# Attention plus ternary feed-forward on one core: the exchange of the values through DRAM in six transfers, two loads and two sums a step sooner

## Chip, core and metric

The kernel runs on one core of one Trainium2 chip. The metric is the device time of one execution in microseconds (us), as the median of several runs. The core has five engines, each with its own in-order queue: TensorE (PE in the profile, its weight loads PEld), VectorE (DVE), ScalarE (ACT), GpSimd (POOL) and SyncE (SP), which here only issues transfers. ACT and POOL issue transfers too. All transfers share 16 DMA engines. An instruction that must wait for a semaphore holds everything behind it on its engine.

## What is computed

```python
def reference(x, Wqkv, Wout, w1, w2, w3):          # x: 1 x 2048 x 256, float32
    xn = layernorm(x)
    q, k, v = heads(einsum('bsd,ed->bse', xn, Wqkv))      # 16 heads of 128
    w = softmax(einsum('bqhd,bkhd->bhqk', q, k) * 128 ** -0.5)
    attn = einsum('bse,de->bsd', einsum('bhqk,bkhd->bqhd', w, v), Wout)
    qz = lambda w: clip(round(w / (mean(abs(w)) + 1e-8)), -1, 1)
    ffn = (sigmoid(xn @ qz(w1).T) * (xn @ qz(w2).T)) @ qz(w3).T
    return x + attn + ffn
```

The factor on the logits makes the softmax sharp, so everything in the attention is in float32.

## The kernel before

**Order of the work.** Layernorm, the first projections and the whole feed-forward come first (about 140 us). Then one loop runs over 64 *blocks*: 16 heads times 4 blocks of 512 queries. A *group* is two heads, so eight blocks; below, i (0 to 7) is the block's number in its group and t (0 to 3) its quarter, and "step (i, t)" names a place in the loop. The order on every engine is written out by hand, step after step; no scheduler moves anything.

**One step.** Each step makes the scores of one tile of 128 queries six steps ahead (`scores`: 16 matmul rows in the trace, maxima on DVE L632, exponentials on ACT L642), moves the exponentials across partitions in 16 transfers (`exchanged`, L661, ten on SP's queue and six on ACT's), turns them in 32 x 32 squares on DVE (`transposed`, L708) and so fills slots of the big tile R. Beside that it computes a quarter of the product of weights and values for block n (`weighted`, L775) and one or two 512-column products for the next heads' projections.

**The product of weights and values** is done by Winograd's scheme for a 2 x 2 partition with 7 products, so sums and differences of both operands are needed. Those of the weights are `differences` on POOL (L728): T1a and T3a of block n+1 in step (n, 3), T1b and T3b in (n, 0), T2l (lower half of the slot) at the end of (n, 0), T2h (upper half) and T4 at the beginning of (n, 1). Quarter 1 of the product reads T1 and T2; its lower half of k needs T2l, its upper half T2h. Those of the values are made once per head by `v_combined` (L750): sums 0 and 1 in step (n, 0) of the head's first block, after T1b and T3b; sums 2 and 3 in (n, 2). Quarter 1 reads sums 0 and 1, quarter 2 reads sum 2.

**Values for the next group.** In blocks 4 to 7 the values of the next two heads are made transposed, half a head at a time, on PE and DVE (L308, L315). To turn them, `v_exchanged` (L317 to L326) moves a half (128 x 1024 numbers, 0.5 MB) across groups of 32 partitions into a scratch area `v_part` (two 128 x 512 pieces, part of the tile xnT), and `v_transposed` (L328 to L333) turns 32 x 32 squares on DVE from there back into the value tile. The same scratch area serves all four halves of a group, so the next exchange has to wait for the turning of the one before. `between` (L1006 to L1048) places these calls at the end of a step: exchanges of the first head at (5, 1) and (7, 1), turned at (5, 3) and (7, 3); exchanges of the second at (5, 3) and (7, 3), turned at (6, 1) and at (0, 1) of the next group.

**Output sums.** The projected output of all heads is accumulated in DRAM tiles `yds`; two of them at a time are loaded into `osums` (`y_moved`, L839), added to on DVE (`fast_o_read`, L911) and stored back. `o_moved` (L846) runs at the end of steps 0 to 3 of blocks 0 to 3 and loads the first of a pair at (0, 0) and (2, 0); the addition that first needs it is in step (0, 1) and (2, 1).

**Other POOL work at these places.** At the beginning of each block `put_away` (L829) stores the finished block from oT, which DVE writes at L803; `spread` (L687) reloads oT with the reciprocals at (n, 1), `inverses` (L680) stores them at (n, 2) in four transfers.

Of the kernel before, what the change touches and what calls it, by code (L numbers as in the profile page):

```python
# [9 lines left out]
F32 = mybir.dt.float32  # L10
# [10 lines left out]
def layernorm_attention_bitffn_kernel(  # L21
# [14 lines left out]
    nc = tc.nc  # L36
    P = 128
    S, DM = x.shape
# [5 lines left out]
    QB = 512  # L44
    NB = S // QB
# [248 lines left out]
    def v_half(h: int, half: int):  # L294
        return v_tile(h)[:, half * NKT // 2 : (half + 1) * NKT // 2]
# [21 lines left out]
    def v_exchanged(h: int, half: int):  # L317

        v = v_half(h, half).rearrange("p k d -> p (k d)")
        for j in range(P // 32):  # L320
            for q in range(P // 32):
                queue = nc.sync if q % 2 else nc.gpsimd
                queue.dma_start(  # L323
                    v_part[q // 2][bass.ts(j, 32), bass.ts(q % 2, S // 8)],
                    v[bass.ts(q, 32), bass.ts(j, S // 8)],
                )  # L326

    def v_transposed(h: int, half: int):  # L328
        v = v_half(h, half).rearrange("p k (q r) -> p q k r", r=32)
        for u in range(2):  # L330
            nc.vector.transpose(  # L331
                v[:, 2 * u : 2 * u + 2], v_part[u].rearrange("p (q k r) -> p q k r", q=2, r=32)
            )  # L333

    wxs, v_part = {}, [xnT[:, 0, bass.ts(c, QB)] for c in (1, 3)]
# [9 lines left out]
    away = ctx.enter_context(tc.tile_pool(name="away", bufs=1, space=bass.MemoryType.DRAM))  # L345
# [2 lines left out]
        [away.tile([P, QB], F32, tag=f"od{h}_{c}", name=f"od{h}_{c}") for c in range(NB)]  # L348
        for h in range(2 * G)
    ]  # L350
    rds = [away.tile([TB, P], F32, tag=f"rd{i}", name=f"rd{i}") for i in range(2)]


# [255 lines left out]
    blocks = [(h, b) for h in range(H) for b in range(NB)]  # L609
# [74 lines left out]
    def spread(n: int):  # L684

        if n < NBK - NB:
            nc.gpsimd.dma_start(oT, rds[n % 2].rearrange("t p -> (t p)").partition_broadcast(P))  # L687
            rbs[n] = oT
# [3 lines left out]
    for n in range(1, len(blocks)):  # L692
        a, b, c, d, e = roles[-1]
# [19 lines left out]
    def differences(n: int, what: str):  # L713

        a, b, c, d, e = roles[n]
        todo, where = what[:2], what[2:]
        o, x, y = {"T1": (e, c, a), "T2": (a, d, e), "T3": (c, d, c), "T4": (b, b, a)}[todo]
        o, x, y = (R[:, i] for i in (o, x, y))
        if where in ("a", "b"):
            t = "ab".index(where)  # L720
            o, x, y = (i[:, t * S // 2 : (t + 1) * S // 2] for i in (o, x, y))
        elif where in ("l", "h"):
            k = "lh".index(where)
            o, x, y = (
                i.rearrange("p (t k q) -> p t k q", t=2 * NQ, q=32)[:, :, k * KH // 2 : (k + 1) * KH // 2]
                for i in (o, x, y)
            )
        nc.gpsimd.tensor_tensor(o, x, y, ALU.subtract)  # L728
# [3 lines left out]
    def v_parts(h: int):  # L732
        if h not in vparts:
            v = v_tile(h)
            k0, k1 = v_place(h, 0), v_place(h, KH)
            ls = [[v[:, k : k + KH, c * HP : (c + 1) * HP] for k in (k0, k1)] for c in range(2)]
            st = apool.tile([P, 3, KH, HP], F32, tag="st", name=f"st{h}", bufs=1)
            s3 = ls[1][0]
            if h == H - 1:
                s3 = wpool.tile([P, KH, HP], F32, tag="wq", name=f"s3{h}")  # L740
            vparts[h] = ls, st, s3
        return vparts[h]

    def v_combined(h: int, i: int):
        ((l11, l12), (l21, l22)), st, s3 = v_parts(h)
        o, x, y, op = (
            (st[:, 0], l21, l22, ALU.add), (st[:, 1], st[:, 0], l11, ALU.subtract),
            (s3, l11, l21, ALU.subtract), (st[:, 2], l12, st[:, 1], ALU.subtract),
        )[i]
        nc.gpsimd.tensor_tensor(o, x, y, op)  # L750
# [75 lines left out]
    def put_away(n: int):  # L826

        h, b = blocks[n]
        nc.gpsimd.dma_start(ods[h % (2 * G)][b], oT)  # L829
# [6 lines left out]
    def o_fetched(g: int, pair: int, i: int, head: int, c: int):  # L836
        nc.gpsimd.dma_start(o3[:, i], ods[(g * G + head) % (2 * G)][2 * pair + c])

    def y_moved(pair: int, c: int, back: bool):  # L839
        y, yd = osums[:, c], yds[2 * pair + c]  # L840
        nc.gpsimd.dma_start(*((yd, y) if back else (y, yd)))

    def o_difference(i: int, a: int, b: int):
        nc.gpsimd.tensor_tensor(o3[:, i], o3[:, a], o3[:, b], ALU.subtract)

    def o_moved(g: int, i: int, t: int):  # L846

        pair, more = i // 2, i == 1
        at = i % 2, t
        if at == (0, 0):  # L850
            o_difference(1, 2, 1)
            y_moved(pair, 0, False)
        elif at == (0, 1):
            o_difference(0, 1, 0)
        elif at == (0, 2):
            o_fetched(g, pair, 2, 1, 0)
        elif at == (1, 0):
            o_difference(2, 2, 1)
            if more:
                o_fetched(g, 1, 0, 0, 0)  # L860
        elif at == (1, 1):
            y_moved(pair, 1, True)
        elif at == (1, 2):
            if more:
                y_moved(1, 1, False)
                o_fetched(g, 1, 1, 0, 1)
            else:
                y_moved(pair, 0, True)
        elif at == (1, 3) and more:
            y_moved(pair, 0, True)  # L870
            o_fetched(g, 1, 2, 1, 1)
            o_difference(1, 1, 0)
# [125 lines left out]
    GB = G * NB  # L998
# [7 lines left out]
    def between(n: int, t: int):  # L1006

        g, i = divmod(n, GB)
        last = NBK - NB

        how = {
            (5, 1): (v_exchanged, 0, 0), (5, 3): (v_transposed, 0, 0), (6, 1): (v_transposed, 1, 0),
            (7, 1): (v_exchanged, 0, 1), (7, 3): (v_transposed, 0, 1),
        }.get((i, t))
        if t == 1:
            spread(n)
            if i == NB - 1 and g + 1 < H // G:
                load_weights(g + 1, "v", nc.gpsimd)
            elif i == GB - 1 and n < last or n == last - 1:
                load_weights(g, "o", nc.gpsimd)  # L1020
        if g and i < NB:
            o_moved(g - 1, i, t)
        elif n < last:
            o_begun(g, i, t)
        if how and g + 1 < H // G:
            how[0]((g + 1) * G + how[1], how[2])
        if n >= last - 1 and t == (1 if n < last else 2):
            b = n + 1 - last
            nc.gpsimd.dma_start(o3[:, b % 2], ods[(H - 2) % (2 * G)][b])
        if g and (i, t) == (0, 1):  # L1030
            v_transposed(g * G + 1, 1)
        if t == 2:
            if i == GB - 1 and n < last:
                wo = weights[g, "o"]
                sums_of(wo[:, :, :P], wo[:, :, P:], f"wos{g}")
        if t == 3:
            if i in (5, 7) and g + 1 < H // G:
                v_exchanged((g + 1) * G + 1, i // 2 - 2)
            if i == NB - 1 and g + 1 < H // G:
                v_sums(g + 1)  # L1040

        b, r = divmod(n * TB + t - ((last - 2) * TB + 1), TB)
        if r == 0 and 0 < b <= NB:
            x_added(b - 1)
        if r == 0 and 0 <= b < NB:
            turning_back(b)
        if r == 2 and 0 <= b < NB:
            turned_back(b)  # L1048

    behind = []  # L1050
    with tc.manual_schedule():
        for u in range(-LEAD, (NBK - 1) * TB):
            n, t = divmod(u, TB)
            v = u + LEAD
# [10 lines left out]
            g, i = divmod(n, GB)  # L1065
            if n >= NB and t < 2:
                i, j = divmod(i, NB)
                j = 2 * j + t
# [19 lines left out]
            if t == 0 and n >= 0:  # L1088
                if 0 < n <= NBK - NB:
                    put_away(n - 1)  # L1090
                differences(n, "T1b")
                differences(n, "T3b")
                if blocks[n][1] == 0:
                    v_combined(blocks[n][0], 0)
                    v_combined(blocks[n][0], 1)
            elif t == 1 and n >= 0:
                differences(n, "T2h")
                differences(n, "T4")
            elif t == 2 and n >= 0:
                if blocks[n][1] == 0:  # L1100
                    v_combined(blocks[n][0], 2)
                    v_combined(blocks[n][0], 3)
            elif t == 3 and -1 <= n < NBK - 2:
                differences(n + 1, "T1a")
                differences(n + 1, "T3a")
            if more:
                scores(v, late=beside)

# [62 lines left out]
        n = NBK - 1  # L1171
# [51 lines left out]
```

## Time and profile before

| | |
|---|---|
| runs | 2405.11, 2409.61, 2410.33 us; median 2409.61 |
| profiled execution | 2405.91 us, span 2403.9 us, mean granted TensorE clock 0.979 |
| busy: PE, POOL, DVE, ACT | 2208.7 (92%), 1824.2 (76%), 1889.2 (79%), 748.0 us (31%) |
| exchange of the values on POOL's queue | 224 issues, 498 ns each, 3.2 us to landing |
| the same on SP's queue | 224 issues, 589 ns each (median), 1.9 us to landing |
| scores start to scores start, steps t = 0 to 3 of block 0 | 13.95, 13.69, 13.02, 6.88 us |
| the same, block 1 | 8.60, 8.60, 8.60, 6.02 us |
| block 2 | 10.16, 9.95, 8.75, 8.82 us |
| block 4 | 8.60, 10.41, 9.77, 6.88 us |
| block 5 | 8.60, 7.75, 8.60, 6.02 us |
| block 6 | 8.72, 10.46, 8.67, 9.38 us |
| block 7 | 8.60, 7.87, 8.60, 6.93 us |

How to read it: the last seven rows are read from the timeline of TensorE as the time between the first score matmuls of neighbouring steps, averaged over blocks 8 to 55 (six groups). In these steps TensorE always has the same scores to do, quarters 0 to 2 of the product are equally long and quarter 3 is half as long; steps differ by at most one extra product of 0.86 us. So 8.60 (or 7.75 with one product fewer) and 6.02 to 6.88 us are steps in which TensorE ran without a gap, and what lies above that is waiting. Engines that are not TensorE may be idle without cost; a wait costs time where it ends up in one of these intervals.

### The profile page before, as it was taken

To read this page: it belongs to the slowest core of one execution; us is meant where nothing else is said; L and a number is where in the kernel's file an instruction comes from. 1 tells how busy PE (TensorE), PEld (TensorE's weight loads), DVE (VectorE), ACT (ScalarE), POOL (GpSimd) and SP (SyncE) were. 2 spreads that over 40 slices of the span, in tenths; PEclk is the share of its full clock that TensorE was granted. 3 is DMA by queue.
4 is the path that set the end of the run, shared out by engine and by line. 5 is a ranking of instruction groups with operands and counts; after the bars stand their busy time and mean duration, and the time that the engine had idled before them with its cause. 6 is when DMAs were issued, how large, how long until landed. Compare 5 with 4: busy or idle time off the path is not lost.

```text
span 2403.9 us, 41619 instructions
## 1 busy us (share of the span) xinstructions
PE 2208.7 (92%) x13386; PEld 1065.3 (44%) x13386; DVE 1889.2 (79%) x2578; ACT 748.0 (31%) x1390; POOL 1824.2 (76%) x1504
## 2 busy tenths in 40 slices
PE   9999999899989999899998999889997999989787
PEld 6644444444434544344443444344443444435345
DVE  6577788788878888788877888778887888878855
ACT  5533333233323333223332333223332333323321
POOL 0166877887797788788788778788778788878984
PEclk9999999999999999999999999999999999999989
DMA  2265656666666666576666766657666665657744
GB/s 85 69 146 149 154 145 175 161 179 166 157 172 184 176 152 163 151 195 174 154 160 153 199 162 153 169 155 184 167 164 154 186 174 149 162 153 190 197 125 126
DMA packets 256170, 383.81 MB, mean 160 GB/s; under 512 B 86224, under 2 KB 97936, under 8 KB 255952
## 3 DMA queue, kind: packets, MB, share of 16 engines
q1 hardware_dynamic: 138416, 182.30, 29.8%
q10 hardware_dynamic: 74896, 101.94, 16.7%
q0 software_dynamic: 42640, 96.92, 14.5%
q8 instruction: 105, 1.72, 0.3%
q14 instruction: 113, 0.93, 0.1%
HBM read 62.98 MB, written 34.73 MB: 41 GB/s over the span
## 4 chain that ended last, share of the span: by engine, by line
PE 28%; DMA 25%; POOL 15%; SPq 11%; DVE 11%; issue 7%; ACTq 2%; ACT 1%; DVEq 0%; POOLq 0%
DMA part<-p 23%; PE av L775 10%; POOL R L728 9%; PE s L94 8%; SPq L661 8%; DVE R L708 5%; SPq L323 3%; DVE mx L632 2%; PE pw L94 2%; POOL st L750 2%; ACTq L661 2%; PE ph L507 2%; DMA xnT<-v 1%; PE pow L94 1%; DVE oU L801 1%
## 5 line engine op out<-in xcount | busy, mean ns | idle before, releaser
L728 POOL TENSOR_TENSOR R<-R 128x1024 f32<-128x1024 f32 x441 | 1180.3, 2684 | 58.2 <-DVE R L708 24.3
L642 ACT ACTIVATE p<-s,nm 128x1024 f32<-128x1024 f32 x512 | 566.8, 1111 | 1458.9 <-DMA part<-p 986.4
L94 PE MATMUL s<-kT,qT 128*64 128x512 f32 x4000 | 926.3, 593 | 11.0 <-ACT p L642 10.9
L632 DVE TENSOR_REDUCE mx<-s 128x1 f32<-128x1024 f32 x512 | 612.2, 1216 | 141.5 <-PE s L94 128.0
L708 DVE STREAM_TRANSPOSE R<-part 128x1024 f32<-128x1024 f32 x512 | 605.7, 1221 | 124.4 <-DMA part<-p 116.4
L775 PE MATMUL av<-R,st 128*64 128x256 f32 x3024 | 515.2, 399 | 106.6 <-POOL R L728 67.1
L775 PE MATMUL av<-R,v 128*64 128x256 f32 x3728 | 553.3, 389 | 25.9 <-DVE oU L801 25.8
L94 PEld LDWEIGHTS s<-kT,qT 128*64 128x64 f32 x4000 | 307.8, 137 | 540.0 <-issue 474.1
L775 PEld LDWEIGHTS av<-R,st 128*64 128x64 f32 x3024 | 302.4, 144 | 320.0 <-POOL R L728 97.3
L775 PEld LDWEIGHTS av<-R,v 128*64 128x64 f32 x3728 | 343.8, 141 | 195.1 <-issue 62.7
L680 POOL DMA_DIRECT2D rd<-r x240 | 124.8, 527 | 135.8 <-DVE r L678 120.8
L911 DVE TENSOR_TENSOR osums<-pow,osums 128x512 f32<-128x512 f32 x196 | 126.0, 678 | 75.6 <-DMA osums<-yd 74.4
L829 POOL DMA_DIRECT2D od<-oT x60 | 34.5, 576 | 170.2 <-DVE oT L803 161.8
L323 POOL DMA_DIRECT2D xnT<-v x224 | 111.7, 505 | 58.3 <-DVE v L331 47.8
L801 DVE TENSOR_TENSOR oU<-av,oU 64x256 f32<-64x256 f32 x248 | 101.1, 408 | 38.0 <-PE av L775 20.1
L793 ACT COPY oU<-av 64x256 f32<-64x256 f32 x248 | 91.0, 367 | 124.5 <-PE av L775 120.4
L642 ACT ACTIVATION_READ_ACCUMULATOR p<-s,nm 128x1 f32 x512 | 100.0, 195 | 0.0
L94 PE MATMUL pw<-t,ws 128*64 128x512 f32 x336 | 94.2, 594 | 2.4 <-DVE kT L200 2.3
L160 POOL TENSOR_TENSOR t<-xnT 128x512 f32<-128x512 f32 x4 | 5.1, 1272 | 106.9 <-DMA part<-p 106.9
L315 DVE TENSOR_TENSOR v<-pvw,v 128x512 f32<-128x512 f32 x98 | 65.1, 676 | 20.6 <-PE pvw L94 20.6
L200 DVE TENSOR_TENSOR kT<-pw,kT 128x512 f32<-128x512 f32 x112 | 76.9, 687 | 1.8
L94 PE MATMUL pw<-xnT,wk 128*64 128x512 f32 x224 | 69.1, 596 | 5.5 <-DVE kT L200 5.2
(164 smaller groups left out, 1606.8 us busy)
## 6 DMA issues: line engine op xcount, KB each, us to landing
part<-p SPq DMA_DIRECT2D x2556, 64.0 KB, 2.2
part<-p ACTq DMA_DIRECT2D x1540, 64.0 KB, 2.3
oT<-rd POOLq DMA_DIRECT2D x60, 256.0 KB, 4.3
od<-oT POOLq DMA_DIRECT2D x60, 256.0 KB, 3.2
o<-od POOLq DMA_DIRECT2D x60, 256.0 KB, 3.8
osums<-yd POOLq DMA_DIRECT2D x28, 512.0 KB, 4.9
yd<-osums POOLq DMA_DIRECT2D x28, 512.0 KB, 4.5
xnT<-v POOLq DMA_DIRECT2D x224, 32.0 KB, 3.2
```

The source lines that it names most:

```text
L94: nc.tensor.matmul(out[c * HP : (c + 1) * HP], lhs[:, c * HP : (c + 1) * HP], rhs, start=start, stop=stop, skip_group_check=True,)
L323: queue.dma_start(v_part[q // 2][bass.ts(j, 32), bass.ts(q % 2, S // 8)], v[bass.ts(q, 32), bass.ts(j, S // 8)],)
L632: nc.vector.tensor_reduce(mx[:, i : i + 1], s, AX.X, ALU.max)
L642: nc.scalar.activation(p, s, AF.Exp, bias=nm, accum_out=sums[n][:, t, i : i + 1],)
L661: queue.dma_start(parts[v][g // 2][bass.ts(j, 32), g % 2, :], ps[j // 2][bass.ts(g, 32), bass.ts(j % 2, S // NQ)],)
L680: nc.gpsimd.dma_start(rds[n % 2][:, bass.ts(j, 32)], riT[32 * j : 32 * j + TB, :])
L708: nc.vector.transpose(to[:, t % 2, 2 * i : 2 * i + 2], part.rearrange("p g (s c) -> p g s c", s=2),)
L728: nc.gpsimd.tensor_tensor(o, x, y, ALU.subtract)
L775: nc.tensor.matmul(av[i * HP : (i + 1) * HP, half], l[:, kk], moving(s, kk), start=start, stop=(k == units[r] - 1), skip_group_check=True,)
L793: nc.scalar.copy(u[op, oq], av[ap, half])
L801: nc.vector.tensor_tensor(u[p, q], av[p, half], u[p, q], ALU.add)
L911: nc.vector.tensor_tensor(y, pm, y, ALU.add)
```

## The change

Three things are changed.

1. `v_exchanged` no longer makes 16 transfers of 32 KB inside SBUF (eight on SP's queue, eight on POOL's). It makes four stores of 128 KB into a new DRAM tile and two loads of 256 KB from it into the scratch area, all six on POOL's queue. A load needs two of the stores to have landed. Every call is one step earlier: exchanges of the first head at (5, 0) and (7, 0), turned at (5, 2) and (7, 2); exchanges of the second at (5, 2) and (7, 2); their turning stays at (6, 1) and (0, 1).
2. The load of the first output sum of a pair moves from the end of step (0, 0) or (2, 0) to its beginning, right behind `put_away` and ahead of T1b.
3. Sums 0 and 1 of a head's values move from (n, 0) to (n-1, 3), behind T1a and T3a, for every head but the first.

```diff
@@ v_exchanged
-        for j in range(P // 32):
-            for q in range(P // 32):
-                queue = nc.sync if q % 2 else nc.gpsimd
-                queue.dma_start(
-                    v_part[q // 2][bass.ts(j, 32), bass.ts(q % 2, S // 8)],
-                    v[bass.ts(q, 32), bass.ts(j, S // 8)],
-                )
+        vd = vds[half].rearrange("(j r) (q c) -> q r j c", r=32, c=S // 8)
+        for q in range(P // 32):
+            nc.gpsimd.dma_start(vd[q], v[bass.ts(q, 32)].rearrange("r (j c) -> r j c", c=S // 8))
+        for u in range(2):
+            nc.gpsimd.dma_start(v_part[u], vds[half][:, bass.ts(u, QB)])
@@ DRAM tiles
+    vds = [away.tile([P, S // 2], F32, tag=f"vd{i}", name=f"vd{i}") for i in range(2)]
@@ o_moved
+    def o_loaded(g: int, i: int):
+        if i % 2 == 0:
+            y_moved(i // 2, 0, False)
+
         if at == (0, 0):
             o_difference(1, 2, 1)
-            y_moved(pair, 0, False)
@@ between
-            (5, 1): (v_exchanged, 0, 0), (5, 3): (v_transposed, 0, 0), (6, 1): (v_transposed, 1, 0),
-            (7, 1): (v_exchanged, 0, 1), (7, 3): (v_transposed, 0, 1),
+            (5, 0): (v_exchanged, 0, 0), (5, 2): (v_transposed, 0, 0), (6, 1): (v_transposed, 1, 0),
+            (7, 0): (v_exchanged, 0, 1), (7, 2): (v_transposed, 0, 1),
...
-        if t == 3:
             if i in (5, 7) and g + 1 < H // G:
                 v_exchanged((g + 1) * G + 1, i // 2 - 2)
+        if t == 3:
@@ the loop over steps
             if t == 0 and n >= 0:
                 if 0 < n <= NBK - NB:
                     put_away(n - 1)
+                if n >= GB and n % GB < NB:
+                    o_loaded(n // GB - 1, n % GB)
                 differences(n, "T1b")
                 differences(n, "T3b")
-                if blocks[n][1] == 0:
+                if n == 0:
                     v_combined(blocks[n][0], 0)
                     v_combined(blocks[n][0], 1)
...
             elif t == 3 and -1 <= n < NBK - 2:
                 differences(n + 1, "T1a")
                 differences(n + 1, "T3a")
+                if n >= 0 and blocks[n + 1][1] == 0:
+                    v_combined(blocks[n + 1][0], 0)
+                    v_combined(blocks[n + 1][0], 1)
```

On POOL's queue the exchange at the end of (5, 0) and (7, 0) stands between T2l and T2h of that block; the one at (5, 2) and (7, 2) stands ahead of T1a and T3a of the next.

## The prediction

> **What bounds the kernel now.** I read the page first: TensorE is busy for 92% of the span and POOL for 76%, so neither a single engine nor the transfers set the pace everywhere. Then the list of waits, for those that name the lines of the change; its columns are who waited, for whom, us in total, times, longest.
>
> ```profile
> PE 2208.7 (92%) x13386; PEld 1065.3 (44%) x13386; DVE 1889.2 (79%) x2578; ACT 748.0 (31%) x1390; POOL 1824.2 (76%) x1504
> ```
>
> ```profile
> PEld av L775 <- POOL R L728: 97.3, 69, 4.6
> ...
> DVE osums L911 <- DMA osums<-yd: 74.4, 14, 9.3
> ...
> PEld av L775 <- POOL st L750: 55.7, 26, 11.6
> POOL xnT L323 <- DVE v L331: 47.8, 13, 6.1
> ...
> DVE v L331 <- DMA xnT<-v: 30.1, 13, 3.3
> ```
>
> All three parts aim at waits that exist: 74.4 us for the output sums, 55.7 for the sums of the values (`st`), 47.8 and 30.1 around the exchange. But DVE's and POOL's waits cost only what reaches TensorE. The step table shows where that is: block 0 loses 13.95+13.69+13.02 against 3 x 8.60, so 15 us; blocks 2, 4 and 6 a few each; blocks 5 and 7 run at full pace. So I followed one such change of heads, steps (23, 0) to (24, 2), on POOL's timeline (columns: start, us, what, count, idle time before it).
>
> ```profile
> 944.43 14.11 POOL L728 TENSOR_TENSOR R<-R 128x1024 f32<-128x1024 f32 x5
> ...
> 960.99 3.48 POOL L323 DMA_DIRECT2D xnT<-v  x7
> 965.26 0.50 POOL L323 DMA_DIRECT2D xnT<-v  x1 [0.79 <-DMA wo<-in_woutT_dram]
> 967.11 2.07 POOL L680 DMA_DIRECT2D rd<-r  x4 [1.36 <-DMA xnT<-v]
> ...
> 980.87 4.03 POOL L323 DMA_DIRECT2D xnT<-v  x8 [4.49 <-DVE v L331]
> ...
> 985.48 4.82 POOL L728 TENSOR_TENSOR R<-R 128x1024 f32<-128x1024 f32 x2
> 990.26 1.27 POOL L750 TENSOR_TENSOR st<-v 128x512 f32<-128x512 f32 x1
> ...
> 1006.89 1.26 POOL L750 TENSOR_TENSOR st<-v,st 128x512 f32<-128x512 f32 x1
> ```
>
> POOL hardly rests from 944.4 until `st` is complete at 1008.15: 63.7 us with 6.6 idle (0.79+1.36+4.49). TensorE waits for it at the end:
>
> ```profile
> 953.96 3.62 PE L775 MATMUL av<-R,st 128*64 128x256 f32 x32
> ...
> 981.68 5.36 PE L775 MATMUL av<-R,v 128*64 128x256 f32 x32 [3.87 <-DVE oU L801]
> ...
> 995.25 2.71 PE L775 MATMUL av<-R,st 128*64 128x256 f32 x16 [2.63 <-POOL R L728]
> 999.33 3.25 PE L775 MATMUL av<-R,st 128*64 128x256 f32 x13 [1.38 <-POOL R L728]
> ```
>
> So in block 0 POOL is the bound, and the 6.5 us that DVE waits for `osums` there run beside POOL's chain.
>
> **The exchange on POOL.** Before, its half costs eight issues, 4.0 us. After, four stores are issued at 0, 0.55, 1.10 and 1.65 us (the 0.55 to 0.58 of L841 and L829). The loads wait on POOL. No row shows such a store; the four carry 512 KB, and one 512-KB store (yd<-osums) lands 4.5 us after its issue, so I let the last land at 5.0; from below, 1.65 plus the 2.2 of a 0.5-KB store (rd<-r) is 3.85; from above, 1.65 plus the longest 256-KB store (od<-oT, 5.0) is 6.65. With the last load's issue, 0.55, POOL is held for D = 5.6 us (4.4 to 7.2). The value is nearest to the row with the same bytes. Not a bound, from a page: the Trainium skill, "DMA: Bandwidth & Descriptors", section "Anatomy of one DMA — SWDGE (gpsimd) path", fits 2.0 us plus bytes over 436 thousand per us; by that estimate a 128-KB store takes 2.3, D would be 4.5 and the sum as in the second rival below. The rows with 256 KB (3.2 us here, 2.6 by the fit) speak for more.
>
> **Its new place at (5, 0) and (7, 0)** is ahead of T2h, T4, `spread`, and at (7, 1) the load of wo and an o difference. T4 and the rest are read 10 us or more later. T2h is not covered: in block 23 the five differences end at 949.2, 951.6, 953.9 (T2h) and 958.5, and quarter 1's second half, which reads T2h, starts at 953.96+3.62/2 = 955.8. In all seven groups T2h is 1.7 to 2.5 us early in blocks 5 and 7. So 5.6-1.8 = **3.8 us of TensorE idle** at (5, 1) and at (7, 1), where there is none now. POOL can't start earlier: its T1b waits for oT of the block before.
>
> **The clock.** The windows view shows what such a gap does: after the 3.87 us gap that ended at 981.68, the granted clock (the column behind the busy times) is 0.51 for a stretch of 3.45 us, and 0.50 again after the gaps at 995 and 999.
>
> ```profile
> 979.00:982.60 3.60, 0.92 (x9) 0.63 (x10) 2.64 (x5) 0.00 (x0) 1.69 (x4) 1.00 0.53 130
> 982.60:986.05 3.45, 3.45 (x20) 1.99 (x18) 3.42 (x5) 0.00 (x0) 3.43 (x7) 0.51 0.82 219
> ```
>
> The 32 matmuls there take 5.36 instead of 3.62 us. So I add 1.7 us to each new gap (0 if a gap falls well in the grid of windows). The Trainium skill, "TensorE: Matmul & The Clock Gate", section "Why this matters for your kernels", warns only of gaps above about 3 us; the 2.63 us here are followed by half clock too. By the page 3.8 us would be charged, a gap of 2.6 not; by the row both.
>
> **Blocks 5 and 6, per group.** Lost: 3.8+1.7. Won: the exchange behind (5, 3) was late for its turning at (6, 1) (part of the 30.1 us), and made DVE late down to (6, 3): 9.38 against 6.88 for the same work in block 4, so 2.5. POOL's `put_away` of block 5 stood 1.9 us behind oT (910.61 against 908.73) because its exchange followed T1a and T3a; now it stands ahead of them, and I work out 1.3 (rd at 899.9 with the shift, 2.1, D, 4.8 of differences end at 912.4 to 913; oT at 911.7): 0.6 won. Net **+2.4**.
>
> **Blocks 7 and 0, per group**, POOL's chain from 944.43 on. T1b to T2l 7.15, D 5.6, T2h and T4 6.95, oT, wo and a difference 2.57: 22.3. rd waits for DVE's reciprocals, which follow TensorE: 964.2-944.43+3.8+1.7 = 25.3. Then rd, o and wos 4.45, D 5.6, T1a and T3a 4.85, the two sums 2.55, put_away and the osums load 1.12, T1b, T3b, T2l 7.15, difference 1.27, T2h and T4 6.95, oT, difference and two sums 4.34: 63.6 against 63.7 now. So the 6.6 idle us that go are given back, to the wait for landing and to TensorE's slip: **-0.1**. The loss at (0, 0) (3.87, DVE's wait for the turning) does vanish, and comes again as a wait for `st` at (0, 2): the two sums have only changed places in POOL's chain, since nothing there is idle in front of them.
>
> **Block 2**: the load at (2, 0) now lands in time, and (2, 3) falls from 8.82 to 6.88, the lateness of DVE behind the 3.8 us wait: **-1.9**. T2h doesn't move, for the 0.55 us issue stays ahead of it. **Block 4** (odd head): here the sums move into idle time, 1.6 us ahead of `put_away`, so T2 comes 1.6 earlier and (4, 1) with its 10.41 wins as much: **-1.6**; they are 2.5 long, so without that cover nothing is won. In the last head POOL is busy with the final transposes on both sides: 0.
>
> **At nothing**: SP loses 8 x 0.59 = 4.7 us of issues per exchange, which shortens DVE's waits for `part`; beyond the 2.5 above these lie beside POOL's chain. From above this is worth 1.7 per group (DVE's wait at (7, 2)), from below nothing. 14.7 MB more traffic: the engines of the transfers are at 64% here; its price is in D's upper end.
>
> **Sum**: 2.4-0.1-1.9-1.6 = -1.2 us per group, times 7 is -8.4. The span 2403.9-8.4 = 2395.5, with the 2.0 us around it **2397.5**; the profiled execution was 3.7 below the median of the runs, which I leave as spread: 2398.
>
> **The rivals.** Each us of D costs 4 per group: one in block 5's stall, one at (6, 1), two in POOL's chain, so 28 in all. *Slower*: D is 7.2 because the stores land late in traffic (od's longest), which holds POOL ahead of T2h. -1.2+1.6 x 4 = +5.2, times 7 is +36: 2442. It decides from D = 5.9 on. For it: 512-KB transfers up to 8.2 us, four stores back to back. Against: POOL's own exchange of 32-KB pieces has its fourth piece land 5.4 us after the first issue, and that among SP's eight. *Much faster*: D is 4.4 and the shorter gaps leave the clock alone. Block 5 and 6: 2.6-2.5-0.6-1.0 = -1.5; POOL's chain: rd at 22.4 instead of 25.3, and 1.2 less, so -4.2; with blocks 2 and 4, -9.2, times 7 is -64: 2342. For it: 2.2 us landings; against: the clock row at 2.63. *The change doesn't do what it says*: POOL is too late for the osums load to help. Against: at (24, 0) it would be issued at about 985.5 and land by 990.4 (4.9 us), wanted at 994.3; small, without block 2's 1.9 it is +5, 2411, inside the others.
>
> **How the numbers follow.** Forecast case, D between 5 and 5.9: 0.45, of which 0.17 lie within 0.2% (4.8 us, about what a measurement can tell); much faster 0.18; slower 0.37. So faster 0.46, same 0.17, slower 0.37. The likeliest case alone is 2380 to 2408; the range, with signs on both sides, 2352 to 2432.
>
> **What would show it.** Right: TensorE's wait for R (L728) grows at (5, 1) and (7, 1) by 3 to 4 us with half clock behind it, the waits for osums and POOL's for L331 vanish, block 0 stays near 45 us, (6, 3) and (2, 3) fall to 6.9, and an exchange holds POOL for 5 to 6 us. Wrong: if T2h stays ahead of quarter 1, if `st` is no longer waited for in block 0, or if the loads' wait is above 3.5 us.

## The result, and the profile after

| | before | after |
|---|---|---|
| median of four runs each | 2407.45 us (2405.11 to 2410.33) | 2430.42 us (2429.28 to 2433.13) |
| ratio, 95% interval | | 1.0097 (1.0079 to 1.0114) |
| span of the profiled execution | 2403.9 us | 2427.9 us |
| mean granted TensorE clock | 0.979 | 0.966 |

The change makes the kernel 1% slower. The forecast was 2398, half a per cent faster, so the sign was wrong; 2430 lies at the upper end of the range, and the case that came true is the rival called *slower*.

The list of waits of after (who waited, for whom, us in total, times, longest) holds the first answer:

```profile
PEld av L774 <- POOL R L727: 151.8, 69, 7.2
...
PE av L774 <- POOL R L727: 118.8, 55, 6.8
...
POOL xnT L324 <- DMA vd<-v: 55.0, 27, 3.2
...
PEld av L774 <- POOL st L749: 49.2, 16, 11.9
...
DVE osums L913 <- DMA osums<-yd: 12.6, 4, 4.1
```

Of the two waits that the small parts aimed at, `osums` fell from 74.4 to 12.6 us, `st` only from 55.7 to 49.2. But TensorE's weight loads now wait 151.8 us for R where it was 97.3, and its matmuls 118.8 where before had:

```profile
PE av L775 <- POOL R L728: 67.1, 58, 4.2
```

And there is a new wait: POOL for its own stores, 55.0 us in 27 waits by this list. The list books part of it under other names: POOL is idle for 97.1 us in all just ahead of the 56 loads of the 28 exchanges, and every one of these loads is issued 0.3 to 0.6 us after the landing of the last store that it needs.

POOL's timeline of after in block 23, steps (23, 0) to (23, 2) (start, us, what, count, idle time before it and who ended it), shows what this wait holds:

```profile
950.58 7.16 POOL L727 TENSOR_TENSOR R<-R 128x1024 f32<-128x1024 f32 x3
957.68 2.23 POOL L322 DMA_DIRECT2D vd<-v  x4
962.62 0.58 POOL L324 DMA_DIRECT2D xnT<-vd  x1 [2.71 <-DMA vd<-v]
963.86 0.56 POOL L324 DMA_DIRECT2D xnT<-vd  x1 [0.66 <-issue]
964.43 6.94 POOL L727 TENSOR_TENSOR R<-R 128x1024 f32<-128x1024 f32 x2
...
982.68 2.25 POOL L322 DMA_DIRECT2D vd<-v  x4
987.30 0.57 POOL L324 DMA_DIRECT2D xnT<-vd  x1 [2.36 <-DMA vd<-v]
988.32 0.56 POOL L324 DMA_DIRECT2D xnT<-vd  x1 [0.46 <-issue]
```

The exchange begins at 957.68 and lets POOL go at 964.42: 6.74 us. T2h comes only then (the first 2.4 us of the 6.94). TensorE's timeline beside it:

```profile
960.11 2.32 PE L774 MATMUL av<-R,st 128*64 128x256 f32 x18
966.84 3.25 PE L774 MATMUL av<-R,st 128*64 128x256 f32 x13 [4.41 <-POOL R L727]
```

Quarter 1 runs until it needs the upper half of R, stands for 4.41 us, and goes on when T2h is there. And the windows view shows the clock behind it (columns: the stretch; busy time and instructions of PE, PEld, DVE, ACT, POOL; granted clock; share of the transfer engines; GB/s): half clock for the next window.

```profile
963.40:966.83 3.43, 0.00 (x0) 0.00 (x0) 0.36 (x1) 0.65 (x2) 2.91 (x2) 0.76 0.76 206
966.83:970.24 3.41, 3.40 (x15) 1.95 (x17) 0.00 (x0) 0.00 (x0) 3.38 (x1) 0.50 0.60 158
```

Over the whole run there are 30 stretches at half clock, 164.7 us together, where before has 23 and 102.6.

The step intervals of TensorE (scores to scores, as in the table before, averaged over blocks 8 to 55) locate the loss. Each cell is the sum over the four steps of the blocks named, in us; the last column is per group against before, over these blocks and blocks 1 and 3.

| | 5 and 6 | 7 and 0 | 2 | 4 | all |
|---|---|---|---|---|---|
| before | 68.2 | 79.5 | 37.7 | 35.7 | |
| after | 73.3 | 82.4 | 35.8 | 33.7 | +3.9 |
| difference | +5.1 | +2.9 | -1.9 | -1.9 | |
| predicted | +2.4 | -0.1 | -1.9 | -1.6 | -1.2 |

Seven times 3.9 is 27, beside 24.0 by the spans. Inside block 5, step (5, 1) went from 7.75 to 13.68; inside block 7, (7, 1) from 7.87 to 13.99. These two make 12.1 us per group, more than the whole loss.

### The profile page after: what moved, and what is told of

Same layout as the page of the kernel before. It is cut to its first block, busy times and chain, and to the rows that moved or that the text cites. A ratio compares the mean times of both kernels' runs of the same rounds, so it can differ in the third digit from the quotient of the medians.

```text
span 2427.9 us, 41301 instructions
## 1 busy us (share of the span) xinstructions
PE 2227.0 (92%) x13386; PEld 1071.3 (44%) x13386; DVE 1903.0 (78%) x2578; ACT 744.5 (31%) x1390; POOL 1812.2 (75%) x1448
## 5 line engine op out<-in xcount | busy, mean ns | idle before, releaser
L94 PE MATMUL s<-kT,qT 128*64 128x512 f32 x4000 | 954.1, 601 | 11.8 <-ACT p L641 11.8
L774 PE MATMUL av<-R,st 128*64 128x256 f32 x3024 | 525.6, 408 | 155.8 <-POOL R L727 118.8
L707 DVE STREAM_TRANSPOSE R<-part 128x1024 f32<-128x1024 f32 x512 | 605.2, 1220 | 29.0 <-DMA part<-p 21.6
L94 PEld LDWEIGHTS s<-kT,qT 128*64 128x64 f32 x4000 | 320.7, 140 | 552.7 <-issue 491.6
L774 PE MATMUL av<-R,v 128*64 128x256 f32 x3728 | 538.0, 381 | 2.4 <-DVE oU L800 2.4
L774 PEld LDWEIGHTS av<-R,st 128*64 128x64 f32 x3024 | 308.3, 146 | 351.7 <-POOL R L727 151.8
L774 PEld LDWEIGHTS av<-R,v 128*64 128x64 f32 x3728 | 332.8, 138 | 186.0 <-issue 67.5
L913 DVE TENSOR_TENSOR osums<-pow,osums 128x512 f32<-128x512 f32 x196 | 125.0, 678 | 12.8 <-DMA osums<-yd 12.6
L324 POOL DMA_DIRECT2D xnT<-vd x56 | 31.6, 564 | 97.1 <-DMA vd<-v 55.0
L94 PE MATMUL pw<-t,ws 128*64 128x512 f32 x336 | 102.7, 592 | 0.0
L843 POOL TENSOR_TENSOR o<-o 128x512 f32<-128x512 f32 x56 | 71.7, 1280 | 0.8 <-DMA o<-od 0.3
```

The costliest lines, as they stand in the source:

```text
L94: nc.tensor.matmul(out[c * HP : (c + 1) * HP], lhs[:, c * HP : (c + 1) * HP], rhs, start=start, stop=stop, skip_group_check=True,)
L707: nc.vector.transpose(to[:, t % 2, 2 * i : 2 * i + 2], part.rearrange("p g (s c) -> p g s c", s=2),)
L774: nc.tensor.matmul(av[i * HP : (i + 1) * HP, half], l[:, kk], moving(s, kk), start=start, stop=(k == units[r] - 1), skip_group_check=True,)
L913: nc.vector.tensor_tensor(y, pm, y, ALU.add)
```

## The experiments

The theory behind all of them: the loss is the time for which one exchange holds POOL, because T2h stands behind it in (5, 1) and (7, 1), and because POOL's chain around the change of heads is full. The runs were made on three chips, each with its own runs of before (medians 2391.62, 2405.70 and 2391.73 us), so ratios are compared. Step intervals come from one profile of each kernel; where they are set beside those of before or after they carry this difference between chips, 0.7% or about 2 us per group, so single small differences in them say little.

### The wait taken away: stores here, loads a step later

```diff
+    def v_loaded(h: int, half: int):
         for u in range(2):
             nc.gpsimd.dma_start(v_part[u], vds[half][:, bass.ts(u, QB)])
...
+        if t in (1, 3) and i in (5, 7) and g + 1 < H // G:
+            v_loaded((g + 1) * G + t // 2, i // 2 - 2)
```

Against after, nothing else is changed: the same six transfers on the same queue, but a step of POOL's other work stands between the stores and the loads.

> The changed kernel with the two loads of each exchange one step behind its four stores: stores at (5, 0), (5, 2), (7, 0), (7, 2), loads at (5, 1), (5, 3), (7, 1), (7, 3). Theory (POOL held for 6.8 us between T2l and T2h is what costs): POOL holds only for the four stores, 2.25 us, which is 0.4 us more than T2h has to spare; blocks 5 and 7 go from 38.1 and 38.9 us back to 31.5 and 32.5, POOL's chain in blocks 7 and 0 gets 7 us shorter than before the change (no waits for landing, no slip of the reciprocals), blocks 2, 4 and 6 stay as in the changed kernel: about -12.9 us per group against before, 2316 us, and in any case below 2360. Rival (the detour through DRAM costs by its traffic, or turning a step sooner does): the same bytes move in the same steps, so it stays within 10 us of the changed kernel, above 2415.

Measured: 2306.78 us, ratio 0.9637 (0.9611 to 0.9662), where 2316 against 2407 would be 0.962. The theory holds, and its rival falls: the same bytes move, and the turning is as early as in after. POOL's and TensorE's timelines of this run at the same place:

```profile
914.46 7.16 POOL L729 TENSOR_TENSOR R<-R 128x1024 f32<-128x1024 f32 x3
921.56 2.23 POOL L322 DMA_DIRECT2D vd<-v  x4
923.80 7.00 POOL L729 TENSOR_TENSOR R<-R 128x1024 f32<-128x1024 f32 x2
...
933.25 1.12 POOL L326 DMA_DIRECT2D xnT<-vd  x2
```

```profile
923.99 3.96 PE L776 MATMUL av<-R,st 128*64 128x256 f32 x31
```

The stores cost POOL their four issues, 2.23 us, T2h starts at once, and the loads at 933.25 find the data landed and wait for nothing. TensorE runs through 31 matmuls where it stood for 4.41 us in after. Steps (5, 1) and (7, 1) are 8.22 and 7.87. POOL's chain from the three differences to the last sum of the values is 914.46 to 970.91, 56.4 us, where before took 63.7. So a wait of a few us, 28 times, makes 4.6% of before's time between after and this version.

### The place and the form, each alone

Three runs fill the table of form (through DRAM, or the 16 direct transfers of before) against place of the first head's exchange ((5, 0) and (7, 0), ahead of T2h, or (5, 1) and (7, 1), behind T4).

Through DRAM, behind T4, against after (the turning stays at (5, 2) and (7, 2)):

```diff
-            (5, 0): (v_exchanged, 0, 0), (5, 2): (v_transposed, 0, 0), (6, 1): (v_transposed, 1, 0),
-            (7, 0): (v_exchanged, 0, 1), (7, 2): (v_transposed, 0, 1),
+            (5, 1): (v_exchanged, 0, 0), (5, 2): (v_transposed, 0, 0), (6, 1): (v_transposed, 1, 0),
+            (7, 1): (v_exchanged, 0, 1), (7, 2): (v_transposed, 0, 1),
```

> The changed kernel with the first head's exchange back at the end of (5, 1) and (7, 1), behind T2h and T4; form, turning and the rest as changed. Theory: TensorE's stalls at (5, 1) and (7, 1) vanish, with them the half clock behind them; POOL is still held 6.8 us per exchange, and DVE waits some 3 us for the turning at (5, 2) and (7, 2). Blocks 5 and 7 at 31 to 33 us, POOL's chain of blocks 7 and 0 about as long as before the change: 2360 to 2375. Rival (DRAM traffic): above 2415.

Direct, ahead of T2h, against after:

```diff
-        vd = vds[half].rearrange("(j r) (q c) -> q r j c", r=32, c=S // 8)
-        for q in range(P // 32):
-            nc.gpsimd.dma_start(vd[q], v[bass.ts(q, 32)].rearrange("r (j c) -> r j c", c=S // 8))
-        for u in range(2):
-            nc.gpsimd.dma_start(v_part[u], vds[half][:, bass.ts(u, QB)])
+        for j in range(P // 32):
+            for q in range(P // 32):
+                queue = nc.sync if q % 2 else nc.gpsimd
...
```

> The changed kernel with the 16 direct transfers of before (eight on POOL, eight on SP) at the new places. Theory (what counts is how long POOL is held ahead of T2h): 4.0 us instead of 6.8, so TensorE waits 2.2 instead of about 5 us at (5, 1) and (7, 1); by 4 us per group for each us, -11 per group against the changed kernel, 2352, less what SP's eight issues take back (up to 20 us over all). Rival (the place alone costs, whatever is issued there): 2430 as in the changed kernel.

Direct, behind T4, is both of these edits together.

> The changed kernel with the 16 direct transfers of before at (5, 1) and (7, 1), (5, 2) and (7, 2); it fills the fourth field of form (direct, through DRAM) by place (ahead of T2h, behind T4). Theory: a direct transfer lands 3 to 4 us after its issue with no store to wait for, so DVE doesn't wait for the turning at (5, 2) and (7, 2) as it does with the DRAM form at this place (4 us), and nothing stands ahead of T2h: 0.975 to 0.98 of before. Rival (the DRAM form is worth its time by sparing SP 224 issues): not below the 0.9925 of the DRAM form at this place.

| ratio to before (95%) | ahead of T2h | behind T4 |
|---|---|---|
| through DRAM | 1.0097 (after) | 0.9925 (0.9905 to 0.9944) |
| direct | 0.9867 (0.9846 to 0.9887) | 1.0087 (1.0058 to 1.0116) |

Neither the form nor the place is the fault by itself; it is what waits for what in each pair.

*Direct, ahead of T2h* (2358.52 us) went the expected way, at the slow edge of what was expected (2352 to 2372 against 2407 is 0.977 to 0.985). The exchange holds POOL for 4.0 us of issues there and waits for nothing; TensorE waits only 1.2 to 1.7 us at (5, 1) and (7, 1), without half clock behind it, (5, 1) takes 9.42, and the mean clock is 0.987.

*Through DRAM, behind T4* (2375.86) has the right sign and about half of the expected gain. The stalls at (5, 1) and (7, 1) are gone (7.85 and 7.75), but the data come too late for the turning one step on. The expectation had this wait of DVE's, some 3 us, but charged TensorE nothing for it (blocks 5 and 7 at 31 to 33 us; they take 36.6 and 38.1). DVE's timeline at the turning of (7, 2), and TensorE's in (7, 3):

```profile
965.32 0.71 DVE L329 STREAM_TRANSPOSE v<-xnT 128x512 f32<-128x512 f32 x1 [2.97 <-DMA xnT<-vd]
966.95 0.71 DVE L329 STREAM_TRANSPOSE v<-xnT 128x512 f32<-128x512 f32 x1 [0.92 <-DMA xnT<-vd]
```

```profile
969.18 1.97 PE L94 MATMUL pw<-xnT,wk 128*64 128x512 f32 x4 [3.97 <-DVE kT L200]
```

DVE stands 3.9 us for the loads; the addition that writes `kT` is behind that on its queue, and TensorE waits 3.97 us for it. The steps (5, 3) and (7, 3) take 11.53 and 13.15 us. So the place behind T4 needs the turning two steps on, as before had it.

*Direct, behind T4* missed: slower than before where it was expected to be faster; its rival, not below the 0.9925 of the form through DRAM, came true. The expectation took the direct form for the quicker one to land. It lands late, since half of it is issued by SP, and SP's queue runs behind. SP's and DVE's timelines, (7, 1) to (7, 3):

```profile
960.02 12.50 SPq L662 DMA_DIRECT2D part<-p  x14
972.56 5.85 SPq L323 DMA_DIRECT2D xnT<-v  x8
```

```profile
979.78 1.30 DVE L331 STREAM_TRANSPOSE v<-xnT 128x512 f32<-128x512 f32 x2 [8.75 <-DMA xnT<-v]
```

POOL issues its eight of the same exchange from 965.35 on; SP begins its eight 7.2 us later, when 14 transfers of the exponentials are out of its queue, and DVE waits 8.75 us for the last. The steps (5, 3) and (7, 3) take 13.80 and 16.96 us. This is what the form through DRAM is good for: it doesn't depend on SP's queue, and so allows the turning a step sooner; but then its own wait must not stand in POOL's way.

### The three parts alone

The exchange alone is before with `v_exchanged`, the DRAM tiles and the places of after (parts 2 and 3 of the change undone).

> The kernel of before with the new exchange and its places alone; osums load and sums of the values as before. Theory: the exchange alone loses more than the whole change does, because blocks 2 and 4 keep their 1.9 us each per group: 2430 + 27 = 2457. Rival (the other two parts bring nothing, since POOL bounds these steps): 2430.

The load of the output sums alone, against before:

```diff
             o_difference(1, 2, 1)
-            y_moved(pair, 0, False)
...
+                if n >= GB and n % GB < NB:
+                    o_loaded(n // GB - 1, n % GB)
```

> The kernel of before with the osums load a step sooner, nothing else. Theory: in block 0 POOL bounds, so DVE's wait there costs nothing; only (2, 3) gets shorter, from 8.8 to 7 us: -1.9 us per group, ratio to before 0.9945. Rival (DVE's 74.4 us of waiting are paid in full): ratio 0.97.

The sums of the odd heads alone, against before:

```diff
-                if blocks[n][1] == 0:
+                if blocks[n][1] == 0 and blocks[n][0] % 2 == 0:
                     v_combined(blocks[n][0], 0)
...
+                if n >= 0 and blocks[n + 1][1] == 0 and blocks[n + 1][0] % 2:
+                    v_combined(blocks[n + 1][0], 0)
+                    v_combined(blocks[n + 1][0], 1)
```

> The kernel of before with sums 0 and 1 of the odd heads (blocks 4 of each group) a step sooner, nothing else. Theory: POOL makes them in the time in which it waits for oT, and (4, 1) falls from 10.4 to 8.6 us: -1.9 us per group, ratio 0.9945. Rival (POOL's order doesn't matter there): 1.000.

The sums of the even heads back in (n, 0), against after:

```diff
-                if n == 0:
+                if blocks[n][1] == 0 and (n == 0 or blocks[n][0] % 2 == 0):
                     v_combined(blocks[n][0], 0)
...
-                if n >= 0 and blocks[n + 1][1] == 0:
+                if n >= 0 and blocks[n + 1][1] == 0 and blocks[n + 1][0] % 2:
```

> The changed kernel with sums 0 and 1 of the even heads (block 0 of a group) back behind T1b and T3b; those of odd heads stay a step sooner. Theory: at this place POOL is busy on both sides, the sums only change places in its chain, so the time is that of the changed kernel, 1.010 of before, within 0.002 (T2l gets 2.5 us later, the sum that quarter 2 waits for stays where it is). Rival (the 55.7 us of waits for the sums were paid in block 0): 7 x 2.5 us slower, 1.017.

| part alone | us | ratio (95%) |
|---|---|---|
| exchange | 2440.86 | 1.0201 (1.0186 to 1.0217) |
| load of the output sums | 2398.89 | 0.9972 (0.9947 to 0.9996) |
| sums of odd heads | 2393.05 | 0.9947 (0.9926 to 0.9969) |
| after, even heads' sums back | 2432.85 | 1.0121 (1.0070 to 1.0173) |

The exchange alone came out at the expected size (2457 against 2407 is 1.021) and is more than the whole loss. The reason given for it holds only in part: block 4 keeps its wait (35.2 us against 33.7 in after), block 2 does not (36.1 against 35.8). The odd heads' sums came as expected in the ratio: (4, 1) falls from 10.41 to 9.01, where 8.6 was expected. Without the move of the even heads' sums block 0 takes 43.32 us, with it 43.45: no difference, as the prediction had it; the interval of the time is too wide to say more.

The load of the output sums brought half of what was expected. The step (2, 3) does fall, from 8.82 to 7.34, but (2, 1) rises from 9.95 to 11.61. DVE's timeline of this run at (1, 3) and (2, 0) shows a wait, 3.76 us at (2, 0), that wasn't in the sum:

```profile
1052.25 2.37 DVE L708 STREAM_TRANSPOSE R<-part 128x1024 f32<-128x1024 f32 x2 [2.32 <-DMA part<-p]
...
1063.37 2.37 DVE L708 STREAM_TRANSPOSE R<-part 128x1024 f32<-128x1024 f32 x2 [3.76 <-DMA part<-p]
```

The transfers of the exponentials (`part`) land later when 512 KB of output sums are loaded beside them. Of those that DVE turns in (2, 0), SP issues the last 6.85 us after the start of the step's scores in both kernels; it lands 2.55 us later in before and 5.26 us later here, where the load is on its way from about 6.4 to 13 us. In the one group of seven in which the load starts only at 9.2 us it lands after 2.2 us. SP's ten for (0, 1) take 3.89 us on average where they took 2.30. DVE's wait at (2, 0) grows from 0.8 to 3.5 us per group, and TensorE waits at (2, 1) for DVE's addition to `osums` behind it. Block 2 as a whole is no shorter (37.8 against 37.7 us); by the steps what the run gained lies in block 0 (46.3 against 47.5), where the expectation had nothing. The rival, by which the whole 74.4 us of DVE's wait would come back as time (0.97), fell.

### How far it goes

With the wait gone, the sums of the values were the last wait of POOL's chain in block 0: (0, 2) takes 13.23 us in the run with the loads a step later, waiting for `st`. So on top of that edit sums 2 and 3 were moved ahead of T4, which is needed later than they are:

```diff
                 differences(n, "T2h")
+                if blocks[n][1] == 0:
+                    v_combined(blocks[n][0], 2)
+                    v_combined(blocks[n][0], 3)
                 differences(n, "T4")
             elif t == 2 and n >= 0:
-                if blocks[n][1] == 0:
-                    v_combined(blocks[n][0], 2)
-                    v_combined(blocks[n][0], 3)
```

> The kernel with the loads a step behind the stores, and on top of it sums 2 and 3 of a head's values between T2h and T4 in (n, 1) instead of in (n, 2). Theory: what is left of block 0's loss is POOL reaching sum 2 late (2.66 us of TensorE idle at (0, 2) and half clock behind it), while T4 isn't needed before (0, 3): (0, 2) falls from 13.2 to about 9 us, 4 us per group, and the last head's wait of some 10 us for the same sums goes too: ratio to before 0.947 to 0.953. Rival (POOL's chain as a whole bounds, in any order): the wait moves to T4 in quarter 3, 0.964 as without it.

And, against the run with the loads a step later, the load of the output sums put back to its place of before:

```diff
             o_difference(1, 2, 1)
+            y_moved(pair, 0, False)
...
-                if n >= GB and n % GB < NB:
-                    o_loaded(n // GB - 1, n % GB)
```

> The kernel with the loads a step behind the stores, but with the osums load back at the end of (0, 0) and (2, 0). Theory: with POOL's chain 7 us shorter, DVE's wait for osums is no longer hidden in block 0: besides (2, 3), step (0, 1) gets longer again, together 3 to 5 us per group, ratio to before 0.973 to 0.979 against 0.964. Rival (the load is worth what it was alone, 0.003): 0.967.

Measured with the sums ahead: 2274.47 us, ratio 0.9456 (0.9414 to 0.9498), the best of all, 5.4% under before and just past the fast end of the expectation. The step (0, 2) is at 8.60, a step without a gap ((0, 3) rises from 6.88 to 8.06), and TensorE is busy for 96% of the span at a clock of 0.992:

```profile
PE 2176.7 (96%) x13386; PEld 1112.8 (49%) x13386; DVE 1902.2 (84%) x2578; ACT 743.9 (33%) x1390; POOL 1807.1 (79%) x1448
```

Stretches at half clock fall to 9 with 37.7 us: TensorE's busy time is 50 us shorter than in after for the same 13386 matmuls.

The other run, loads a step later but the output sums loaded at their old place, gave 2310.88 us, ratio 0.9666 (0.9622 to 0.9711). It missed the expectation of 0.973 to 0.979 and fits the rival: beside the faster POOL chain the earlier load is worth about the 0.003 that it is worth alone. By the steps it is (2, 3), 8.76 against 7.46 us with the load early; block 0 is the same (38.5 against 38.4).

## Why the prediction was wrong, point by point

**The step that failed** is the price of the wait: "so I let the last land at 5.0", and from it D = 5.6 us. Over the 28 exchanges of after the last store lands 5.74 us after the first issue, POOL issues the load 0.54 us after that landing, and the issue takes 0.56: D is 6.83 us on average (5.92 to 7.63). Of the 1.28 us that were missing (against 5.0 + 0.55), 0.74 are the landing and 0.54 the time from landing to issue, for which the sum had no term at all. Every one of the 28 holds is above 5.9, the point from which the prediction let the slower rival decide. The profile's groups of the stores and loads show the sizes (out<-in, operation, count, KB, median us to landing):

```profile
vd<-v POOLq DMA_DIRECT2D x112, 128.0 KB, 3.9
xnT<-vd POOLq DMA_DIRECT2D x56, 256.0 KB, 4.2
```

The last of the four stores takes 4.05 us from its own issue, where the 5.0 left it 3.35. The Trainium skill, "DMA: Bandwidth & Descriptors", section "Anatomy of one DMA — SWDGE (gpsimd) path", fits 2.3 us to a store of this size; the last of four in a row took 1.8 times that here, so the measurement decides, and against the fit. Whether the row or the other traffic makes it so long was not separated.

A row of before could have told of it. The prediction set POOL's own exchange of 32-KB pieces, whose fourth piece lands 5.4 us after the first issue, against the slow case. Over the 28 exchanges of before the first four have landed 5.0 us after the first issue on average (3.5 to 6.7): four in a row already took the 5.0 that was allowed for four times the bytes.

**The rest of the sum held, with the right D put in.** The prediction charged 4 us per group for each us of D: 4 x 1.23 = 4.9, and -1.2 + 4.9 = +3.7 per group, times 7 is +26, so a span of 2430 against 2427.9 measured. Also by place: blocks 5 and 6, +2.4 + 2 x 1.23 = +4.9 (measured +5.1); blocks 7 and 0, -0.1 + 2 x 1.23 = +2.4 (measured +2.9). The mechanism of the loss, T2h behind the exchange with half clock after the stall and a POOL chain that gives the wait on, was right; the size of one term turned the sign. That the sum comes out this close is partly luck, as the next paragraphs show. The bounds did hold it (4.4 to 7.2), but the value taken inside them came from a single 512-KB store instead of from several in a row.

Step by step it fits less well: (6, 3) fell to 7.53 and (2, 3) to 7.51 where 6.9 was predicted, and (5, 2) and (5, 3) lost 1.2 that were in no term, while the stall at (5, 1) cost 5.9 and not the 6.7 that 3.8 + 1.7 + 1.2 would give. Block 6 won 2.1 us, where 3.1 less the 1.2 that the longer D costs there would be 1.9. These differences cancel to within 0.2 us in the sum of blocks 5 and 6.

**Block 2: right number, cause right only in part.** -1.9 was put down to the earlier load of the output sums, and -1.9 was measured. The load does shorten (2, 3): in all runs that have it early this step takes 7.3 to 7.5 us, in all that have it late 8.5 to 8.8, so 1.3 of the 1.9. But (2, 1) gives part of that back (9.95 to 10.51), the load alone leaves block 2 at 37.8, and the exchange alone, with the load at its old place, brings it to 36.1. The rest is at (2, 0), which falls from 10.16 to 9.18, and follows SP's queue. In before SP issues its last transfer of the exponentials that DVE turns in (1, 3) 7.7 us after ACT has issued its own last one, and DVE waits 2.1 us for it; in after it is 3.7 us, and DVE doesn't wait. The four runs with SP 7.5 to 7.9 us behind there have (2, 0) at 10.2 to 10.7 us, the eight with 3.5 to 4.0 at 8.8 to 9.6. One of the eight is the direct form behind T4: SP has its 224 issues there too, but TensorE's long step (7, 3), 16.96 us, leaves it time to catch up. This points at SP being behind, and not at the form of the exchange by itself; no run changed SP's queue alone.

**At nothing.** SP's relief was priced at nothing, from above at 1.7 us per group. Nothing was too low. DVE's waits for the exponentials fall from 116.4 us in before to 21.6 in after:

```profile
DVE R L708 <- DMA part<-p: 116.4, 99, 4.0
```

```profile
DVE R L707 <- DMA part<-p: 21.6, 50, 3.7
```

With the same places, the form through DRAM without its wait has a ratio of 0.9637, the direct form 0.9867. Part of these 0.023 is POOL's shorter hold, 2.2 us of stores and a step later 1.1 of loads against 4.0 of issues; but of the 6.6 us per group by which their steps differ, 2.5 lie in block 2, where neither has an exchange. How much of the rest is SP's was not separated.

**Block 4** was right in number and in the main in cause: -1.6 predicted, -1.9 measured, and the odd heads' sums alone give (1 - 0.9947) x 2405.7 / 7 = 1.8; the exchange alone takes another 0.5 off this block. **Block 0** was right: the loss at (0, 0) shrinks (13.95 to 9.72), and `st` is waited for at (0, 2) instead, as TensorE's timeline of after shows in (24, 2).

```profile
1017.27 0.43 PE L774 MATMUL av<-R,st 128*64 128x256 f32 x1 [2.62 <-POOL st L749]
```

**The clock** was charged rightly at (5, 1) and (7, 1): the 4.41 us gap is followed by a window at 0.50, as are the other 13 gaps there, of 3.4 to 6.8 us. But the reading that a gap of 2.63 us is charged too does not hold in general. The 2.62 us gap just shown, with the same length, is followed by full speed in the windows view of after:

```profile
1014.20:1017.60 3.40, 0.78 (x7) 0.26 (x6) 3.13 (x7) 2.27 (x4) 3.40 (x4) 1.00 0.78 193
1017.60:1021.20 3.60, 3.60 (x34) 2.24 (x32) 1.44 (x3) 0.03 (x1) 2.36 (x6) 1.00 0.48 95
```

The Trainium skill, "TensorE: Matmul & The Clock Gate", section "Why this matters for your kernels", names only idle gaps above about 3 us. The gap of 4.41 and this one of 2.62 agree with it, the one of 2.63 in before does not. Between 266 and 2290 us of both traces, all 27 gaps of 3.0 us and more are followed by half clock, 10 of 16 of those from 2.0 to 3.0 us in before and 5 of 12 in after, the shortest 2.1. What tells the short ones apart was not tried.

**What should have told of it.** The prediction said that a wait of the loads above 3.5 us would show it wrong. That sign was badly chosen: the longest single wait in the list is 3.2, and the hold is 6.83 all the same, for the wait is split over two loads (2.70 and 0.76 us of idle time on average), and the list gives part of it other names: the longest idle time before a load is 3.84. The hold has to be read from the timeline, from the first store's issue to the next work behind the last load.

## What to carry to other kernels

A write and a read-back through DRAM on one in-order queue cost the issuing engine the whole landing here, 6.83 us each time, against 2.2 us of stores and 1.1 of loads with other work of it between the two. Put the stores at the first place and the loads where their data have landed: the same six transfers went from 1.0097 to 0.9637 of the old time. When a term of the sum decides the sign and no row shows it, take the value that several transfers in a row suggest, and count the time from landing to the next issue; and look in the issuing queue for what stands behind the wait, since that was what TensorE paid for. Then order a full engine's chain by when each result is read: two sums ahead of one difference were worth another 1.8%.

## What the runs showed of the hardware

- A load on POOL that waits for a store to land was issued 0.54 us after the landing, on average over 28 exchanges.
- Four 128-KB stores issued 0.56 us apart: the last took 4.05 us to land, all together 5.74 from the first issue.
- Two gaps of TensorE of the same length, 2.63 us in before and 2.62 in after, were followed by a granted clock of 0.50 and of 1.00; all 27 gaps of 3.0 us and more between 266 and 2290 us of the two traces were followed by 0.50.
- SP's queue of transfers ran 7.2 us behind POOL's in block 23 of the direct form behind T4, so transfers placed at the same step began that much later. In before SP was still 7.7 us behind ACT's part of the same transfers at (1, 3), eight steps after its last exchange.
- Other transfers land later beside a 512-KB load: 5.26 us after issue against 2.55 at (2, 0), and 3.89 against 2.30 at (0, 1).
